# Layer 3's expert results sent to the tokens' rows block by block, and layer 0's attention written in two parts a batch

## The chip, the cores and the metric

The kernel runs on one core of one Trainium2 chip. The metric is device time in microseconds (us) of one execution: the median of several. Engines are named as in the profile: PE (TensorE matmul), PEld (TensorE weight load), DVE (VectorE), ACT (ScalarE), POOL (GpSimd) and SP (SyncE, which here only issues transfers). Each engine runs its instructions in the order in which they stand in its stream.

## The reference

Four layers, each a cross-attention and an expert network, both added to `x` (4 batches of 512 tokens, 128 wide, all float32). The context has 154 rows of 128 a batch. Layer 0's attention and layer 3's experts are what the change rewrites most:

```python
# layer 0: one score matrix, softmax over the context, and one summary of the tokens
Sim = (hc @ w1)[:, :, None] + (hq @ w2)[:, None, :] + einsum('bid,bjd->bij', hc * w3, hq) + b_sim[0]
hq_hat = einsum('bij,bjd->bid', softmax(Sim, axis=2), hq)
hc_bar = einsum('bi,bid->bd', softmax(max(Sim, axis=2), axis=1), hc)[:, None, :]
x = x + concatenate([hc, hq_hat, hc * hq_hat, hc * hc_bar], -1) @ W_qv + b_qv     # hc = layernorm(x), hq = context
# layer 3's experts: 8 experts, the two best of each token, 128 -> 512 -> 128
top_vals, top_idx = top_k(logits, 2)                       # logits = xn @ W_router + b_router
w = softmax(the two values)
out = sum over the token's two experts e of  w[e] * (relu(xn @ W1[e] + b1[e]) @ W2[e] + b2[e])
x = x + out                                                # this is the kernel's output
```

Layers 0 and 2 also send each token to two experts, layer 1 to one. Layers 1 to 3 have attention with 16 heads.

## The kernel before

`x` stays in SBUF, 4 batches with 4 groups of 128 tokens each. The expert networks work in two halves of two batches (1,024 tokens). For a half, `route` (L650 to L807) computes the logits, finds the experts, counts tokens per expert with matmuls of triangular matrices, and gives every (token, choice) a slot `su` so that the tokens of an expert lie together and every expert starts at a multiple of 128. `scatter` (L722) is one indexed transfer of POOL for 128 tokens and one choice: it writes their normalised rows `xn` to the DRAM array `buf` at the slots. With two choices a half has 16 scatters. `experts` (L825 to L946) then runs over blocks of 128 slots: 23 blocks a half where there are two choices, 15 in layer 1. It loads four blocks of `buf` at a time (`tok`, L840), transposes them (L850), loads the weights of the block's expert from DRAM (`w<-in_up`, L862 and L869), multiplies up (L877), applies the activation (L900 to L912), multiplies down (L916), copies the result to `ys` (L925) and stores it to the DRAM array `ybuf` (L928). `gather` (L948) queues 16 indexed reads on POOL (L953), one for 128 tokens and one choice, each of which waits for all stores of its half, and `combine` (L964) adds the rows, times their weights, to `x` (L971).

Indexed transfers are put in a list, `rows_due`, and started by `row_transfers` (L641) from places in the other work, a few at a time; each such place makes them wait for one of its instructions, which spreads them over that work.

The order of the engines' work comes from three sources. Much of it is laid down by a scheduler, which orders the program's instructions for each engine. The attention of layers 1 to 3 (`attend_all`, L1296) is under a manual order: periods, one per 128 tokens, in which PE and ACT (and from layer 2 on DVE) follow the program's order. Generators with `yield` cut `route`, `experts` and the combining of half 1 into steps, which are called from within other work (`Steps`).

The halves overlap: half 1's route runs beside half 0's experts, half 0's gathers beside half 1's experts, half 1's gathers beside the first periods of the next layer's attention. After layer 3 there is nothing beside half 1's gathers.

Layer 0's attention differs: `prepare` (L1002) computes the scores of a batch and `tile_of` (L1026 to L1083) the rest: transposed softmax `pm` and `pt`, the product `hq`, the maximum over all tokens `mall`, the exponentials `ebt`, the summary `hc`, and twelve matmuls with W_qv (L1078) into `res`. `attend_first` (L1278) runs the four batches, with half 0's route after the second and its 16 scatters beside the third and fourth. After it the transposes of layer 1's weights are issued (L1097 to L1108).

In the main loop (L1346 on), SP's queue carries the loads of tokens and weights, the stores to `ybuf`, and in layer 3 the output stores `out_x` (L1392 for half 0, L1403 for half 1).

Of the kernel before, what the change touches and what calls it, by code (L numbers as in the profile page):

```python
# [9 lines left out]
F32 = mybir.dt.float32  # L10
I32 = mybir.dt.int32
# [18 lines left out]
NH = NT // 2  # L30
EPS = 1e-5
NEG = -1e20
BLK = (2 * NH + E - 1, NH + E - 1)
UPS = (2, 1, 1, 1)
NF = (4, 4, 2, 4)
PER = (1, 2, 2, 2)


# [9 lines left out]
def tile_xattn_moe_stack(ctx: ExitStack, tc: tile.TileContext, a: dict, out: bass.AP):  # L48
# [73 lines left out]
    upper = const.tile([P, P], F32, name="upper")  # L122
# [22 lines left out]
    nc.gpsimd.memset(wide_ends, 0.0)  # L145
# [4 lines left out]
    for base, sign in ((0, 1), (D // H - 1, -1)):  # L150
# [17 lines left out]
    fill = const.tile([P, E, NH], F32, name="fill")  # L168
    nc.gpsimd.iota(
        fill, pattern=[[0, E], [P, NH]], base=0, channel_multiplier=0, allow_small_or_imprecise_dtypes=True  # L170
# [6 lines left out]
    nth = const.tile([1, BLK[0], E], F32, name="nth")  # L177
    nc.gpsimd.iota(
        nth, pattern=[[1, BLK[0]], [0, E]], base=0, channel_multiplier=0, allow_small_or_imprecise_dtypes=True
# [59 lines left out]
    def norm(src, found, pool=None):  # L239
        mv, rstd = found  # L240
        xn = (pool or xnp).tile([P, NI, D], F32, tag="xn", name="xn", bufs=3 if pool else 2)
        for i in range(NI):
            nc.vector.tensor_scalar(
                xn[:, i, :], src[:, i, :], mv[:, i, 0:1], rstd[:, i : i + 1], ALU.subtract, ALU.mult
            )
        return xn

    def transposed(xn, gamma=None, beta=None):
        q = ps_tr()
        for i in range(NI):  # L250
            nc.tensor.transpose(q[:, i * P : (i + 1) * P], xn[:, i, :], ident)
# [18 lines left out]
    class Tile:  # L270
# [31 lines left out]
        def exp(self, g):  # L302
            if g == 0:
                self.pr = p2.tile([P, H, S2], F32, tag="probs", name="probs")
            for s in range(min(3, 8 - 3 * g)):
                for j in range(2):
                    h = self.at.heads(None, 3 * g + s, j)
                    nc.scalar.activation(  # L308
# [5 lines left out]
                    )  # L314

        def short(self):
            if self.nb == 1:
                self.ends = p2.tile([P, 4, T4], F32, tag="short", name="short", bufs=1)
# [41 lines left out]
        def take_ends(self, engine):  # L360
            self.tails = p2.tile([self.rows, 4, P], F32, tag="tails", name="tails")
            copy(engine, self.tails.rearrange("p g q -> p (g q)"), self.q["ends"][0 : self.rows, :])
# [173 lines left out]
    def attention64(b, gather_x, wq, wk, wv, wo, add):  # L536
# [36 lines left out]
        def values_ends():  # L573
# [3 lines left out]
            for r in range(2):  # L577
                rows = slice(64 * r, 64 * r + 64)
                nc.tensor.matmul(q[rows, :], ct2[:, b], wv[:, r * 512 : (r + 1) * 512], start=True, stop=True)
# [6 lines left out]
            at.vt = at.vt.rearrange("p c s d -> p (c s d)")  # L586

# [35 lines left out]
    def rsm(name, *shape, dt=F32):  # L623
        return rt.tile([P, *shape], dt, tag=name, name=name)

    def top(lg):

        m = rt.tile([P, NH], F32, tag="m", name="m", bufs=4)
        nc.vector.tensor_reduce(m, lg, AX.X, ALU.max)
        eq = rt.tile([P, NH, E], F32, tag="eq", name="eq", bufs=4)  # L630
        nc.vector.tensor_tensor(eq, lg, bc(m, 2, E), ALU.is_equal)
        nc.vector.tensor_tensor(eq, eq, bc(rev_e, 1, NH), ALU.mult)
        r = rt.tile([P, NH], F32, tag="r", name="r", bufs=4)
        nc.vector.tensor_reduce(r, eq, AX.X, ALU.max)
        oh = rt.tile([P, NH, E], F32, tag="oh", name="oh", bufs=4)
# [5 lines left out]
    def row_transfers(n=2 * NH, behind=None):  # L641
# [5 lines left out]
        del rows_due[:n]  # L647

    seen = []

    def route(layer, half, wg, bg, b2):

        lg = rsm("lg", NH, E)
        found = [stats(x[2 * half + k]) for k in range(B // 2)]
        yield
        xns = [norm(x[2 * half + k], found[k], rt) for k in range(B // 2)]
        yield  # L660
        xnTs = [transposed(xn) for xn in xns]
        yield
        for k, xnT in enumerate(xnTs):
            q = ps_tr()
            for i in range(NI):
                nc.tensor.matmul(q[:, i * E : (i + 1) * E], xnT[:, i * P : (i + 1) * P], wg, start=True, stop=True)
            o = lg[:, k * NI : (k + 1) * NI, :]
            qv = q[:, 0 : NI * E].rearrange("p (i e) -> p i e", i=NI)
            if bg is None:
                nc.vector.tensor_copy(o, qv)  # L670
            else:
                nc.vector.tensor_tensor(o, qv, bc(bg, 1, NI), ALU.add)
        yield
# [3 lines left out]
        sel = rsm("sel", NH + 1, E, dt=BF16)  # L677
        nc.vector.memset(sel[:, NH, :], 0.0)
        if layer == 1:
            nc.vector.tensor_copy(sel[:, 0:NH, :], oh1)  # L680
        else:
            yield
            lg2 = rsm("lg2", NH, E)
# [3 lines left out]
            nc.vector.tensor_tensor(sel[:, 0:NH, :], oh1, oh2, ALU.add)  # L687
# [3 lines left out]
        n = (NH + 1) * E  # L691
        q = ps_tr()
        nc.tensor.matmul(q[:, 0:n], before, sf, start=True, stop=False)
        for s in range(1, NH + 1):
            nc.tensor.matmul(q[:, s * E : n], ones_b, sf[:, 0 : n - s * E], start=False, stop=(s == NH))
        rk = rsm("rk", NH + 1, E)
        nc.vector.tensor_copy(rk, q[:, 0:n].rearrange("p (t e) -> p t e", t=NH + 1))
        tot = rk[:, NH, :]
        t3 = rsm("t3", E, NH)
        nc.vector.tensor_tensor(t3, bc(tot, 2, NH), fill, ALU.is_gt)  # L700
        nb = rsm("nb", E)
        nc.vector.tensor_reduce(nb, t3, AX.X, ALU.add)
        t4 = rsm("t4", E, E)
# [4 lines left out]
        base = rsm("base", NH, E)  # L708
        nc.vector.scalar_tensor_tensor(base, bc(first, 1, NH), float(P), rk[:, 0:NH, :], ALU.mult, ALU.add)
        slots = []  # L710
        for k, oh in enumerate(ohs):
            t5 = rsm("t5", NH, E)
            nc.vector.tensor_tensor(t5, base, oh, ALU.mult)
            sl = rsm(f"sl{k}", NH)
            nc.vector.tensor_reduce(sl, t5, AX.X, ALU.add)
            su = rsm(f"su{k}", NH, dt=U32)
            nc.vector.tensor_copy(su, sl)
            slots.append(su)
        scatters = []

        def scatter(t, su):
            ins = nc.gpsimd.indirect_dma_start(  # L722
                out=buf[half],
# [10 lines left out]
        rows_due.extend(partial(scatter, t, su) for t in range(NH) for su in slots)  # L734
# [698 lines left out]
```

## Time and profile before

| | |
|---|---|
| median of 3 runs | 1352.45 us (1351.14 to 1359.07) |
| the profiled execution | 1282.47 us |
| its span, first to last instruction | 1280.8 us |
| mean granted TensorE clock in it | 0.917 of full speed |
| layer 0: attention; experts | about 20 to 104; 106 to 262 us |
| layer 1: attention; experts | about 260 to 500; to 560 us |
| layer 2: attention; experts | about 560 to 800; to 895 us |
| layer 3: attention; experts | about 895 to 1140; 1144 to 1251 us |
| the end: last `ys` to the end of the span | 1251.4 to 1280.8 us |
| bytes moved by DMA | 126.77 MB, mean 99 GB/s |

The profile is one execution, taken by the hardware profiler. It gives for every engine its busy time and number of instructions; for each group of instructions (a line of the kernel, an engine, an operation, and the tiles it writes and reads, out<-in) the busy time, the mean time of one in ns, the idle time of the engine ahead of it, and what ended most of that; and a chain, followed back from the last instruction to what released each one. In a timeline the first number is the start in us from the beginning of the span, the second the duration. "issue" is time in which an engine waited for nothing that the profile shows; SPq and POOLq are the instruction queues of SP and POOL that issue transfers. The profiled execution is 70 us shorter than the median of the runs.

### The profile page before, as it was taken

Reading aid. Unit: us, or ns where it says so; the run is one execution under the profiler, and the core shown is the slowest. Engines: PE = TensorE matmul, PEld = TensorE weight load, DVE = VectorE, ACT = ScalarE, POOL = GpSimd, SP = SyncE. Lnnn points to the kernel's source line nnn. Section 1 sums busy time; section 2 is a strip of 40 time slices with the busy share of each in tenths; the row PEclk is TensorE's granted clock in tenths of the full one; section 3 lists DMA queues with packets and bytes.
Section 4 is the critical chain, followed back from the end, with each engine's and each line's share of the span. In section 5 each row is a group of like instructions: output and inputs, shape, how many; then the busy total and the mean of one; then the engine's idle time right before and its main releaser. Section 6 shows DMA issues by size and latency. Waiting matters only on the chain.

```text
span 1280.8 us, 26318 instructions
## 1 busy us (share of the span) xinstructions
PE 1089.4 (85%) x9351; PEld 896.9 (70%) x9351; DVE 731.6 (57%) x2012; ACT 565.3 (44%) x2264; POOL 253.6 (20%) x281
## 2 busy tenths in 40 slices
PE   4787998977878888889999998966899999899990
PEld 3657998933435448787878777855778788789890
DVE  6554646567666763335665776424476576646352
ACT  2113433454554543546656565321656665532230
POOL 2041315023000010232000004045220000402334
PEclk8767999988898988998999999887999999999996
DMA  7023786721100314433112214444421111334762
GB/s 228 1 81 113 216 253 189 207 94 25 23 19 26 100 38 119 133 110 84 35 35 55 64 37 123 123 150 133 127 55 45 41 35 35 109 95 143 209 191 60
DMA packets 136064, 126.77 MB, mean 99 GB/s; under 512 B 12538, under 2 KB 115583, under 8 KB 135551
## 3 DMA queue, kind: packets, MB, share of 16 engines
q1 hardware_dynamic: 128767, 110.39, 30.5%
q0 software_dynamic: 7168, 14.69, 3.9%
q8 instruction: 77, 1.26, 0.4%
q14 instruction: 52, 0.43, 0.1%
HBM read 101.31 MB, written 23.72 MB: 98 GB/s over the span
## 4 chain that ended last, share of the span: by engine, by line
PE 59%; DVE 12%; DMA 9%; issue 8%; ACT 5%; POOL 5%; SPq 2%; POOLq 0%; DVEq 0%
PE sc L877 11%; PE av L916 6%; PE tr L371 6%; PE sc L607 5%; PE av L408 5%; PE tr L425 5%; PE sc L592 3%; DMA yg<-ybuf,su 3%; POOL yg L953 3%; ACT probs L308 3%; DVE nm L294 3%; PE sc L1175 2%; DMA w<-in_up 2%; PE av L390 2%; PE tr L358 2%
## 5 line engine op out<-in xcount | busy, mean ns | idle before, releaser
L308 ACT ACTIVATE probs<-sc,nm 128x154 f32<-128x154 f32 x768 | 286.9, 403 | 162.7 <-DVE nm L294 162.5
L877 PE MATMUL sc<-tokT,w 128*128 128x128 f32 x1528 | 201.3, 286 | 8.7 <-DMA w<-in_up 3.6
L877 PEld LDWEIGHTS sc<-tokT,w 128*128 128x128 f32 x1528 | 189.0, 200 | 15.5 <-ACT eg L900 5.2
L294 DVE TENSOR_REDUCE nm<-sc 128x6 f32<-128x924 f32 x144 | 142.6, 1007 | 74.8 <-PE sc L607 49.1
L308 ACT ACTIVATION_READ_ACCUMULATOR probs<-sc,nm 128x1 f32 x768 | 168.3, 219 | 0.0
L916 PE MATMUL av<-w,hT 128*128 x1160 | 155.3, 279 | 3.2 <-DVE hT L905 2.5
L953 POOL DMA_INDIRECT yg<-ybuf,su x112 | 106.7, 952 | 246.5 <-ACT pT L267 59.9
L722 POOL DMA_INDIRECT buf<-xn,su x112 | 109.6, 979 | 227.0 <-DVE eb L745 97.3
L916 PEld LDWEIGHTS av<-w,hT 128*128 128x128 f32 x1160 | 141.9, 193 | 8.9 <-issue 4.7
L236 POOL TENSOR_TENSOR rstd<-ve,nhalf 128x4 f32<-128x4 f32 x32 | 33.0, 1032 | 547.3 <-DVE ve L234 429.6
L264 DVE COPY pT<-tr 128x512 f32<-128x512 f32 x160 | 106.9, 684 | 45.3 <-PE tr L371 41.5
L408 PE MATMUL av<-pT,vm 128*64 128x128 f32 (+1 forms) x1536 | 106.2, 284 | 22.5 <-DVE pT L264 22.4
L371 PE MATMUL tr<-ident,probs 128*128 128x128 f32 x768 | 123.1, 291 | 1.5 <-DVE rT L337 1.5
L371 PEld LDWEIGHTS tr<-ident,probs 128*128 128x128 f32 x768 | 86.1, 146 | 33.4 <-issue 21.7
L408 PEld LDWEIGHTS av<-pT,vm 128*64 128x64 f32 (+1 forms) x1536 | 63.8, 126 | 55.7 <-DVE pT L264 30.9
L900 ACT ACTIVATE eg<-sc,w 128x128 f32<-128x128 f32 x184 | 52.9, 368 | 89.5 <-PE sc L877 82.1
L607 PE MATMUL sc<-kT,qT 64*128 64x154 f32 x1024 | 87.1, 308 | 4.8 <-ACT probs L308 4.8
L905 DVE SCALAR_TENSOR_TENSOR hT<-sc,w,eg 128x128 f32<-128x128 f32 x184 | 56.2, 342 | 51.0 <-ACT eg L900 51.0
L607 PEld LDWEIGHTS sc<-kT,qT 64*128 64x128 f32 x1024 | 71.3, 189 | 15.8 <-issue 9.9
L592 PE MATMUL sc<-xnT,wq 128*128 128x128 f32 x512 | 73.6, 303 | 4.7 <-ACT probs L308 2.3
L592 PEld LDWEIGHTS sc<-xnT,wq 128*128 128x128 f32 x512 | 67.3, 212 | 10.2 <-issue 3.6
L425 PE MATMUL tr<-wo,aT 128*128 128x128 f32 x512 | 66.2, 284 | 1.6 <-DVE xnT L256 1.3
(255 smaller groups left out, 1432.2 us busy)
## 6 DMA issues: line engine op xcount, KB each, us to landing
w<-in_up SPq DMA_DIRECT2D x46, 516.0 KB
w<-in_up SPq DMA_DIRECT2D x76, 258.0 KB
rep<-rd SPq DMA_DIRECT2D x64, 256.0 KB
tok<-buf SPq DMA_DIRECT2D x36, 256.0 KB
ybuf<-ys SPq DMA_DIRECT2D x58, 128.0 KB
w<-in_down SPq DMA_DIRECT2D x3, 2048.0 KB
w<-in_up SPq DMA_DIRECT2D x46, 128.0 KB
ybuf<-ys SPq DMA_DIRECT2D x52, 64.0 KB
```

The lines of the kernel that those rows point to most:

```text
L264: return nc.vector.tensor_copy(o, i)
L294: nc.vector.tensor_reduce(self.at.heads(self.nm, g, n), self.sc[g][:, :, 0 : n * S2].rearrange("p j (s k) -> p j s k", s=n), AX.X, ALU.max ...
L308: nc.scalar.activation(self.pr[:, h, :], self.sc[g][:, j, s * S2 : (s + 1) * S2], AF.Exp, bias=self.nm[:, h : h + 1], accum_out=self.rs[:, ...
L371: nc.tensor.transpose(q[:, t * P : (t + 1) * P], self.pr[:, h, 0:P], ident)
L408: nc.tensor.matmul(av[rows, cols], v, self.pT[n][:, t, :], start=False, stop=last)
L425: nc.tensor.matmul(o[:, 0:D], self.aT[:, c, :], self.at.wo[:, c, :], start=(c == 0), stop=(c == self.nb - 1))
L592: nc.tensor.matmul(sc[:, c // 4, c % 4 * P : (c % 4 + 1) * P], wq[:, c * P : (c + 1) * P], at.xnT[:, i * P : (i + 1) * P], start=True, sto ...
L607: nc.tensor.matmul(sc[:, j, s * S2 : (s + 1) * S2], at.qT[i][rows, c, :], at.kT[rows, c, :], start=True, stop=True)
L722: ins = nc.gpsimd.indirect_dma_start(out=buf[half], out_offset=bass.IndirectOffsetOnAxis(ap=su[:, t : t + 1], axis=0), in_=xns[t // NI][:, ...
L877: nc.tensor.matmul(dst, w[:, b, at : at + P], xT, start=True, stop=True)
L916: nc.tensor.matmul(y[:, b * D : (b + 1) * D], hT[:, fc, :], w2[:, bass.ds(es[b], 1), fc, :].rearrange("p o d -> p (o d)"), start=(fc == 0) ...
L953: ins = nc.gpsimd.indirect_dma_start(out=yg[:, t, :], out_offset=None, in_=ybuf[half], in_offset=bass.IndirectOffsetOnAxis(ap=su[:, t : t ...
```

## The change

It has four parts.

*Layer 3's results.* A row that is sent to the experts is two floats longer in layer 3 (130 instead of 128): the first is the token's row number in an array by tokens, two rows a token, less 4096; the second is the slot of its first choice. These rows go to DRAM arrays of their own, `last`, which are cleared by two more stores at SP. When the experts read a group of blocks, DVE compares the slot in each row with the slot at which it lies (`other` is 1 where it is the token's second choice) and computes `goal`, the row of (token, choice); a slot that no token filled has a goal beyond the array. Each block's `ys` is sent to the rows `goal` of `by_token` by one indexed transfer of POOL with a bounds check, which leaves out the rows beyond the array. These are listed in `results_due` and started up to six pairs of blocks late (`LAG`; layer 3 works on two blocks at a time, and a `ys` holds both), and `ys` has 8 buffers instead of 3. `sums` reads a batch with one plain load of 512 KB at SP, adds both choices to `x`, and stores the output. `ybuf`, its stores, and the gathers fall away in layer 3.

*Layer 0's attention.* `tile_of` is a generator with one `yield` after `ebt`; `attend_first` puts its halves and the steps of half 0's route in a manual order for PE. The route works batch by batch in layer 0. The matmuls of `hq` come after the transpose of the maximum. Each spot starts 4 scatters instead of 2. The route of half 1 has its first step in `attend_first`. The set-up of layer 1's attention (its weights' transposes) comes after half 0's experts instead of ahead of them.

*Gathers of layers 0 to 2.* The gathered rows are in tiles of one batch (6 buffers) instead of a half (2), and a batch's sums follow when its own gathers have been started. In layer 1's first period each group of exponentials starts three gathers, and the second period takes a step of the combining.

*Buffers.* Fewer buffers for several small tiles of the route and for `tails`; four for the normalised rows of the route; one tile for layer 0's gates; `short` shares the memory of `wide_ends`, whose clearing moves to after layer 1's attention; in layer 1 the parts that prepare the next batch's keys and queries come one period later.

The core of the diff:

```diff
@@ experts
+        loaded, toks, goals = {}, {}, {}
+        buf = bufs[layer == 3][half]
...
+            if layer == 3:
+                other = small.tile([P, 4], F32, tag="other", name="other")
+                nc.vector.tensor_tensor(
+                    other[:, 0:m], tok[:, 0:m, D + 1], slot[:, 4 * g : 4 * g + m], ALU.not_equal
+                )
+                goal = small.tile([P, 4], U32, tag="goal", name="goal", bufs=6)
+                nc.vector.scalar_tensor_tensor(
+                    goal[:, 0:m], tok[:, 0:m, D], float(ROWS), other[:, 0:m], ALU.add, ALU.add
+                )
+                goals[g] = goal
...
-            ys = p3.tile([P, 2, D], F32, tag="ys", name="ys")
-            row_transfers(
-                2 * n, nc.vector.tensor_copy(ys[:, 0:n], y[:, 0 : n * D].rearrange("p (b d) -> p b d", b=n))
+            ys = p3.tile([P, 2, D], F32, tag="ys", name="ys", bufs=LAG + 2)
+            done = nc.vector.tensor_copy(ys[:, 0:n], y[:, 0 : n * D].rearrange("p (b d) -> p b d", b=n))
+            some = min(len(rows_due), 2 * n)
+            row_transfers(some, done)
+            if layer == 3:
+                results_due.extend(partial(result, j, ys[:, b, :]) for b, j in enumerate(blocks))
+                results(4 - some)
+                results(len(results_due) - LAG * n)
+            else:
+                rows = ybuf[half][blocks[0] * P : (blocks[0] + n) * P, :]
+                stores.append(nc.sync.dma_start(rows.rearrange("(b p) d -> p b d", p=P), ys[:, 0:n]))
+
+        def result(j, y):
+            ins = nc.gpsimd.indirect_dma_start(
+                out=by_token[half],
+                out_offset=bass.IndirectOffsetOnAxis(ap=goals[j // 4][:, j % 4 : j % 4 + 1], axis=0),
+                in_=y,
+                in_offset=None,
+                bounds_check=ROWS - 1,
+                oob_is_err=False,
             )
-            rows = ybuf[half][blocks[0] * P : (blocks[0] + n) * P, :]
-            stores.append(nc.sync.dma_start(rows.rearrange("(b p) d -> p b d", p=P), ys[:, 0:n]))
...
@@ after gather and combine
+    def sums(half, routed, stores):
+        batches = GROUPS[3][half]
+        def get(b):
+            yg = p2.tile([P, NI, 2, D], F32, tag="k", name="yg2")
+            rows = by_token[half][2 * b * S : 2 * (b + 1) * S, :].rearrange("(i p c) d -> p i c d", p=P, c=2)
+            wait_for(nc.sync.dma_start(yg, rows), stores, "any block may hold these tokens")
+            return yg
+        for k, yg in enumerate([get(b) for b in batches]):
+            b = batches[k]
+            for i in range(NI):
+                t = k * NI + i
+                xi = x[b][:, i, :]
+                for c, (cw, _) in enumerate(routed[1]):
+                    nc.vector.scalar_tensor_tensor(xi, yg[:, i, c, :], cw[:, t : t + 1], xi, ALU.mult, ALU.add)
+            nc.sync.dma_start(out_v[b], x[b])
+            yield
...
@@ Tile.exp
+            if self.at.dh < 64 and self.at.first and self.i == 0:
+                row_transfers(3, ins)
...
@@ attend_first
-        tiles = [prepare(b, found[b]) for b in range(2)]
-        tiles[0](0)
-        tiles.append(prepare(2, found[2]))
-        tiles[1](0)
-        beside = Steps(route(layer, 0, *gates[layer])).step(3)
-        tiles.append(prepare(3, found[3]))
-        beside.step(5)
-        tiles[2](0)
-        beside.step(1)
-        tiles[3](0)
-        return beside.finish()
+        first, second = (Steps(route(layer, half, *gates[layer])) for half in range(2))
+        with tc.manual_schedule(engines={mybir.EngineType.PE}):
+            tiles = [prepare(b, found[b]) for b in range(2)]
+            tiles[0].finish()
+            tiles.append(prepare(2, found[2]))
+            tiles[1].step()
+            first.step()
+            tiles[1].finish()
+            tiles.append(prepare(3, found[3]))
+            tiles[2].step()
+            first.step(3)
+            tiles[2].finish()
+            first.step(2)
+            tiles[3].step()
+            first.step(2)
+            tiles[3].finish()
+            first.finish()
+            second.step()
+        return first.result, second
...
@@ main loop
+        if layer == 3:
+            second = Steps(experts(layer, 1, routed[1], w2))
+            while len(stores) < most_blocks(layer, 0):
+                second.step()
+            got = Steps(sums(0, routed[0], stores))
+            while not (second.done and got.done):
+                second.step(2)
+                got.step()
+            results()
+            Steps(sums(1, routed[1], second.result)).finish()
+            break
+        got = gather(layer, 0, routed[0], stores)
+        if layer == 0:
+            prepare = setups[1]()
+        at = prepare(0, found)
```

## The prediction

> **What bounds the kernel now.** I read the page from the top: engine shares, the chain that ended last, then the costliest groups; after that the chain by time, the timeline and the busy time by stretch for the three places that the change touches.
>
> ```profile
> PE 1089.4 (85%) x9351; PEld 896.9 (70%) x9351; DVE 731.6 (57%) x2012; ACT 565.3 (44%) x2264; POOL 253.6 (20%) x281
> ...
> PE 59%; DVE 12%; DMA 9%; issue 8%; ACT 5%; POOL 5%; SPq 2%; POOLq 0%; DVEq 0%
> ...
> L953 POOL DMA_INDIRECT yg<-ybuf,su x112 | 106.7, 952 | 246.5 <-ACT pT L267 59.9
> L722 POOL DMA_INDIRECT buf<-xn,su x112 | 109.6, 979 | 227.0 <-DVE eb L745 97.3
> ```
>
> TensorE carries 59% of the chain, and its work is all but unchanged. What can move is the rest, and it sits in few places: POOL's 5% is nearly all gathers. One indexed transfer occupies POOL 0.95 us, and the timeline has the next start 1.25 us (gather) or 1.265 us (scatter) later. The end of the chain by time:
>
> ```profile
> 1249.28 1.80 PE av L916 x16
> 1251.43 2.79 DMA ybuf<-ys
> 1254.68 0.49 issue
> 1255.38 0.95 POOL yg L953
> 1256.63 0.94 POOL yg L953
> ...
> 1273.83 0.30 issue
> 1274.13 2.40 DMA yg<-ybuf,su
> 1276.63 0.35 DVE x L971
> ```
>
> TensorE is done at 1251.1; then a store, 16 gathers in a row, one landing, a multiply-add and the output store: 1280.8 - 1251.4 = 29.4 us with TensorE idle. The busy times by stretch (busy and number of PE, PEld, DVE, ACT, POOL; granted clock; DMA share; GB/s) say the same, and show the two other places:
>
> ```profile
> 75.00:100.00 25.00, 23.76 (x107) 18.86 (x107) 11.27 (x43) 2.33 (x7) 13.99 (x15) 0.59 0.28 99
> ...
> 270.00:305.00 35.00, 22.38 (x178) 10.85 (x178) 26.18 (x72) 15.84 (x78) 16.39 (x17) 0.94 0.15 38
> ...
> 1200.00:1250.00 50.00, 47.23 (x391) 45.93 (x392) 23.99 (x77) 14.11 (x47) 15.20 (x16) 0.97 0.74 216
> 1250.00:1281.00 31.00, 1.07 (x10) 0.88 (x8) 6.77 (x20) 0.00 (x0) 15.13 (x16) 0.60 0.21 58
> ```
>
> Layer 0's attention (75 to 100) runs TensorE busy but at clock 0.59; layer 0 to 1 (270 to 305) leaves TensorE idle 12.6 of 35 us beside 16 gathers; the last experts (1200 to 1250) are full, but DMA is at 0.74.
>
> **What the Trainium skill says.** "DMA: Bandwidth & Descriptors", section "Anatomy of one DMA", puts a fixed cost of about 2 us on each DMA, most of it the receipt of the write. The trace agrees: last gather 2.40 us from issue to use, last scatter before layer 0's experts 2.25. Its section "Issuing engines are not separate DMA queues" says that DMAs of SP and POOL run on the same 16 engines: result scatters compete with the weight loads of the last experts, which at 0.74 have a quarter left. Its section "How a descriptor splits into AXI transactions" counts more beats for rows that don't begin at 256 B: 520-byte rows do so; no run here shows such rows. "TensorE: Matmul & The Clock Gate", Part 1, has the clock at half after an idle window of about 3.4 us; the 0.59 above and the 0.60 of the tail fit.
>
> **Part 1: layer 3's tail.** Gone: 28 SP stores ybuf<-ys and 32 gathers. New: 46 result scatters (23 a half) on POOL, four loads of 512 KB on SP, 24 DVE operations on four columns (nearest: 0.15 to 0.2 us each, 4 us together, beside a DVE that is idle half of that stretch: 24.0 busy of 50). A result with a bounds check is in no row of this trace; the nearest is L722 with 0.96 busy and 1.265 apart. Lower bound: rows out of bounds are dropped, say 0.9; upper: half as much again, 1.9 apart. I take 1.265. Experts give a block every 2.0 to 2.3 us (23 in 46.3 us, PE 1204.6 to 1250.9), so POOL keeps up at 1.265 and just at 1.9.
> After the last ys, the instruction order leaves the last pair or so of results (3 x 1.265 = 3.8), a landing 2.4, the two loads (1 MB together; tok loads of 256 KB take 2.7 to 2.8, so 4 to 6), multiply-adds of the second batch (8 x 0.35 = 2.8) and the output store 3.8: 16.8 to 18.8 instead of 29.4. **Saved: 10.6 to 12.6.**
>
> **Part 2: what it costs ahead of the tail.** POOL between the halves now runs 10 results, 12 scatters, 2 results, 4 scatters. Before, the 16 scatters ran 1177.0 to 1197.0 without a hole, and the chain goes through the last one (1196.05), its landing and tok's load (1198.44, 2.84). Two results in between: 2 x 1.265 = 2.5; rows of 520 B: 0 to 1, I take 0.5. So the second half's experts start 3 us later. Then SP: the loads yg2 of half 0 wait for all 23 results (last issued near 1212.7, landed near 1215) and stand in SP's order ahead of the expert weights of later blocks; the two output stores stand there as well. Behind them: w<-in_up, then TensorE. Before, this place wasn't free either: the chain runs gathers, x L971, SPq L1392, w<-in_up from 1213 to 1233, some 4 us of TensorE idle time. I take 1 us more than before, between -2 (half 0's sums are ready sooner than gathers that end at 1232.8) and +6. **Cost: 4 us (1 to 10). Layer 3 net: -7.5 (-12 to 0).**
>
> **Part 3: layer 0's attention.** TensorE's order is written by hand, and half 0's route is spread over it. The number of matmuls stays. Before, a tile took 13 to 15 us, the route sat between 54.6 and 72.3 with TensorE often idle (14.6 busy of the 25 us from 50 to 75), and tile 3 ended at 98.5. I estimate 86 for tile 3 after: the 10.4 idle us filled, and some 2 us from an earlier start. But the experts wait for the 16 scatters, not for tile 3: first scatter 72.78, last 101.17 with the end in 103.4. In the new order the slots `su` come after tile 2 instead of before it; counting DVE's work ahead of them, near 81. From there 16 x 1.265 = 20.2, landing 2.3: 103.5 to 104. **The gain is swallowed: 0,** between -8 (su at 73 and no spreading) and +4 (su behind tile 3's work on DVE). Layer 1's weight transposes (L1099 to L1108) move behind half 0's experts; in the chain they held wo_r's load for 1.8 us at 91.84, which is part of the gain that scatters hide. The first steps of half 1's route also move ahead of the experts, under the scatters.
>
> **Part 4: layer 0 to 1.** The 16 gathers of half 1 ran from 274.1 to 301.1, spread by their order; three are now issued at each exp group of the first tile. Their condition, stores ending at 269.2, stays. 16 x 1.25 = 20 from there: the last starts at 288 and not 300. TensorE's idle time of 4.5 us before L358 at 304.76, for the residual behind x L971, should go; but DVE, in order, takes the combines in front of the second tile's maxima, and waits for gathers there instead, up to about 6 us. Net -1.5 (-6 to +4). Layers 1 to 2 and 2 to 3 keep their order; per-batch tiles let batch 0's sums go earlier: 0 (-2 to +1).
>
> **Costed at nothing.** Two more clears of 1.5 MB on SP's queue, in the 32 us slice that moved 1 GB/s near 32 to 64, before the first expert weights at 73: cover 30 us; without it, 3 MB at about 200 GB/s would delay weights by 15 us. Fewer buffers (eq, tails, route tiles): each is written again a tile later, 12 us on; gone cover would show as DVE waits of about 0.3 us. memset of wide_ends moves to POOL after layer 1's attention, where it is idle.
>
> **Sum.** -7.5 + 0 - 1.5 - 0.5 (a bit of Part 3's earlier work) = -9.5 us on the profiled execution of 1282.47 (span 1280.8 and 1.67 around it). That lies 70 us below the median of 1352.45. What I change is idle time set by DMA and POOL, which a slower TensorE does not stretch, so I carry over microseconds and not a ratio: 1352.45 - 9.5 = **1343 us.**
>
> **Rivals.**
> 1. *Forecast (0.50):* tail shortened, the rest about even: -4 to -13.
> 2. *All parts pay (0.28):* su comes near 74, so that layer 0's experts start 7 us sooner, and layer 1's start gains its 4.5: -8 - 7 - 4 = -19, 1333. For it: 10.4 us of idle TensorE in 50 to 75. Against it: 20 us of scatters on POOL remain after su.
> 3. *Slower (0.17):* SP's queue stalls the last experts. If half 0's results land late (price 1.9 apart: 23 results and 16 scatters take 64 us from 1157, to 1221 and later), yg2's loads and the output stores hold the weights behind them, each w load being 4 us from issue to use. It decides from a stall of about 12 us, three weight pairs late one after the other; with 16 us lost, and layer 1's combines 5 us late, it is +10: 1362. For it: SPq is in the chain there already, DMA 0.74 busy. Against it: three pairs of weights are loaded ahead.
> 4. *The tail doesn't shorten (0.05):* results lag, and POOL holds 10 of them at the end: 12.6 us instead of 3.8, leaving 2 us of gain, about 1350.
>
> A measurement of this kernel can tell about 1% (13.5 us) from no change. Forecast -9.5 lies inside this; of case 1 about a quarter lies beyond -13.5, with the sizes' errors, of case 2 nearly all: faster by over 1% 0.38, within 0.51, slower 0.11. Range: down to 1328 for case 2 with its bounds, up to 1359 to take in most of case 3.
>
> **What would show it.** Right: after the last ys, at most four result scatters, two loads and the store in 16 to 19 us; the first experts' tok load at 103 to 105 although tile 3 ends before 90; gathers of layer 0's half 1 in one row from 269 to 289. Wrong: experts of layer 0 starting before 99; PE idle for more than 8 us in 1205 to 1255 with SP holding w<-in_up behind yg2; result scatters over 1.3 us apart; DVE waiting over 8 us for gathers at layer 1's start.

## The result, and the profile after

The changed kernel is slower: 1363.59 us (median of 20 runs, 1351.95 to 1377.62) against 1353.8 (20 runs, 1342.29 to 1360.08), ratio 1.0078, interval 1.0058 to 1.0098. The prediction had 1343 (1328 to 1359). A ratio here is the time of a kernel over that of the kernel before in the same set of runs, with its 95% interval.

Sets of runs on different chips came at two levels of time: the kernel before took 1355.0 us (median) on the chip that the record numbers 10, 1278.4 and 1280.1 on chips 12 and 14, and the set above, whose chip isn't recorded, is of the upper level; the profile that the prediction was read from (span 1280.8) is of the lower. The ratio of the changed kernel is the same at both (a second set, at the lower level, gave 1.0080 with 1.0054 to 1.0107), but the places where it loses are not quite the same. The profiles below are of the lower level unless the text says otherwise.

The page of the changed kernel, in the parts shown of before:

```profile
PE 1084.9 (85%) x9351; PEld 893.2 (70%) x9351; DVE 730.4 (57%) x2044; ACT 564.9 (44%) x2264; POOL 267.9 (21%) x297
...
PE 54%; DVE 15%; issue 10%; DMA 9%; POOL 5%; ACT 5%; SPq 0%; POOLq 0%; DVEq 0%; ACTq 0%
```

TensorE's busy time is within 0.5% of before, but its share of the chain fell from 59% to 54%. DVE's share rose from 12% to 15% with its busy time unchanged: DVE is more often the one that the others wait for. The tail, by the chain in order of time:

```profile
1264.69 0.98 POOL by_token L1007
...
1268.65 2.12 DMA by_token<-ys,goal
...
1270.99 3.45 DMA yg<-by_token
1274.44 0.03 issue
1274.46 3.50 DVE x L1092 x13
```

From the last result to the end of the span it is what was forecast: three results, a landing, two loads, sums, the store; 16.1 us from the last ys instead of 29.7. These 13.6 us are gained. What is lost ahead of it, the time from one kind of block to the next shows. Each entry is the time from the row above, taken at the first and last `ys` copy (DVE) of each half of experts (h0, h1); "changed" is its second profiled execution, and the last three columns are experiments:

| to | before | changed | late goals | + scatters first | + no early gathers |
|---|---|---|---|---|---|
| layer 0, end of h1 | 261.7 | 264.3 | 262.3 | 264.5 | 262.4 |
| layer 1, start of h0 | 229.9 | 230.4 | 228.6 | 234.7 | 225.0 |
| layer 1, end of h1 | 82.5 | 85.6 | 85.1 | 89.0 | 88.1 |
| layer 2, end of h1 | 332.3 | 331.2 | 331.5 | 331.8 | 331.7 |
| layer 3, start of h0 | 249.9 | 254.6 | 248.1 | 248.1 | 248.0 |
| layer 3, end of h0 | 48.6 | 44.9 | 43.8 | 48.8 | 48.8 |
| layer 3, start of h1 | 7.5 | 16.8 | 16.8 | 6.1 | 6.0 |
| layer 3, end of h1 | 38.7 | 38.5 | 38.9 | 41.2 | 41.2 |
| end of the span | 29.7 | 16.1 | 16.7 | 16.5 | 16.4 |

The profiles of before and of the changed kernel are 1.6 us apart and not 10: the changed one is the shortest of its six runs, the one of before lies 2 to 4 us above the medians of its level. In the same way "late goals" is the shortest of its 11 runs and "+ scatters first" one of the longest of its 22. What differs by several us between executions with the same code is the first three rows, so they are not read alone; the layer 3 rows repeat within 0.6 us in a second profile of the kernel before at this level (`before_third`, below). In them the tail gains 13.6, and the four rows ahead of it lose 10.1: layer 3 is 3.5 us ahead, where 7.5 was forecast, and layers 0 to 2 are behind, by 5.2 us in these two profiles and by more in the medians.

At the upper level layer 3's loss sits elsewhere: its half 0 takes 65.9 us in the changed kernel's first profile and 53.8 in a kernel that has layer 3's results as before (`l3_old`, below); the three other rows ahead of the tail add up to less than 1 us, and the tail gains 12.5. In that half DVE has two waits, of 8.5 and 9.6 us, that the profile puts down to something "remote"; `l3_old` has one of 8.7, on ACT. What that is stays open (last section).

```profile
1252.83 1.13 DVE L979 TENSOR_SCALAR hT<-sc,w 128x128 f32<-128x128 f32 x4 [8.47 <-remote]
1271.76 1.13 DVE L979 TENSOR_SCALAR hT<-sc,w 128x128 f32<-128x128 f32 x4 [9.56 <-remote]
```

Two waits stand out in the changed kernel. From the table of waits, engine, line and what it waited for, with total us, times, longest:

```profile
DVE other L913 <- DMA tok<-last: 22.3, 10, 6.0
```

And DVE's timeline in the last periods of layer 3's attention:

```profile
1135.12 0.69 DVE L286 COPY pT<-tr 128x512 f32<-128x512 f32 x1
1139.84 0.16 DVE L913 TENSOR_TENSOR other<-tok,slot 128x4 f32<-128x4 f32 x1 [4.02 <-DMA tok<-last]
1139.91 0.68 DVE L286 COPY pT<-tr 128x512 f32<-128x512 f32 x1
1140.52 0.15 DVE L917 SCALAR_TENSOR_TENSOR goal<-tok,other 128x4 uint32<-128x4 f32 x1
```

and TensorE's:

```profile
1136.48 0.66 PE L395 MATMUL tr<-ident,probs 128*128 128x128 f32 x4
1140.65 1.12 PE L432 MATMUL av<-pT,vm 128*64 128x128 f32 x8 [3.52 <-DVE pT L286]
```

The goal's first instruction takes 0.16 us and waits 4.02 us for the load of the rows (3.31 us, from 1136.50), which itself waits for the last scatter (1133.99, landed after 2.37). Behind it in DVE's order stands a copy of the attention (`pT`), and for that TensorE waits 3.52 us. It is most of the 4.7 us more in the row "layer 3, start of h0". The second wait is on POOL, between the halves:

```profile
1203.36 0.96 POOL L777 DMA_INDIRECT last<-rows,su  x1 [0.30 <-issue]
1204.62 0.99 POOL L1007 DMA_INDIRECT by_token<-ys,goal  x1 [0.30 <-issue]
1205.92 0.98 POOL L1007 DMA_INDIRECT by_token<-ys,goal  x1 [0.31 <-issue]
1207.20 0.96 POOL L777 DMA_INDIRECT last<-rows,su  x1 [0.30 <-issue]
...
1210.99 0.95 POOL L777 DMA_INDIRECT last<-rows,su  x1 [0.30 <-issue]
```

Twelve scatters, two results, four scatters: half 1's rows are complete only after the last scatter. TensorE's first transpose of them, in the kernel before and in the changed one:

```profile
1201.32 0.91 PE L850 MATMUL tr<-ident,tok 128*128 128x128 f32 x4 [2.39 <-DMA tok<-buf]
1217.23 1.97 PE L906 MATMUL tr<-ident,tok 128*128 128x128 f32 x8 [6.31 <-DMA tok<-last]
```

### The profile page after: what moved, and what is told of

It is laid out like the page before. It is cut to its first block, busy times and chain, and to the rows that moved or that the text cites. A ratio compares the mean times of both kernels' runs of the same rounds, so it can differ in the third digit from the quotient of the medians.

```text
span 1350.0 us, 26336 instructions
## 1 busy us (share of the span) xinstructions
PE 1107.2 (82%) x9351; PEld 904.4 (67%) x9351; DVE 728.3 (54%) x2044; ACT 564.8 (42%) x2264; POOL 268.9 (20%) x297
## 4 chain that ended last, share of the span: by engine, by line
PE 55%; DVE 16%; issue 10%; DMA 8%; ACT 5%; another core or an unknown queue 4%; POOL 2%; SPq 1%; POOLq 0%; DVEq 0%; ACTq 0%
PE sc L944 10%; PE av L985 7%; PE tr L395 6%; PE av L432 5%; PE sc L632 5%; PE tr L449 4%; ACT probs L330 3%; DVE nm L316 3%; PE sc L1300 2%; PE sc L617 2%; DMA w<-in_up 2%; PE av L414 2%; DMA yg<-ybuf,su 2%; PE tr L382 2%
## 5 line engine op out<-in xcount | busy, mean ns | idle before, releaser
L944 PE MATMUL sc<-tokT,w 128*128 128x128 f32 x1528 | 205.1, 287 | 20.5 <-DMA w<-in_up 8.1
L985 PE MATMUL av<-w,hT 128*128 x1160 | 165.5, 287 | 31.0 <-issue 21.2
L985 PEld LDWEIGHTS av<-w,hT 128*128 128x128 f32 x1160 | 148.6, 198 | 40.6 <-issue 26.0
L432 PE MATMUL av<-pT,vm 128*64 128x128 f32 (+1 forms) x1536 | 109.1, 287 | 28.0 <-DVE pT L286 25.9
L1050 POOL DMA_INDIRECT yg<-ybuf,su x80 | 77.1, 964 | 219.7 <-issue 62.0
L777 POOL DMA_INDIRECT buf<-rows,su x80 | 77.6, 970 | 167.5 <-DVE ve L255 54.9
L432 PEld LDWEIGHTS av<-pT,vm 128*64 128x64 f32 (+1 forms) x1536 | 64.4, 128 | 63.2 <-DVE pT L286 38.1
L632 PE MATMUL sc<-kT,qT 64*128 64x154 f32 x1024 | 88.8, 312 | 4.8 <-ACT probs L330 4.8
L993 DVE COPY ys<-av 128x256 f32<-128x256 f32 (+1 forms) x110 | 38.8, 355 | 84.8 <-PE av L985 43.1
L974 DVE SCALAR_TENSOR_TENSOR hT<-sc,w,eg 128x128 f32<-128x128 f32 x184 | 56.1, 342 | 45.4 <-ACT eg L969 45.3
L449 PE MATMUL tr<-wo,aT 128*128 128x128 f32 x512 | 70.8, 296 | 2.4 <-DVE xnT L278 1.3
```

The lines of the kernel that those rows point to most:

```text
L432: nc.tensor.matmul(av[rows, cols], v, self.pT[n][:, t, :], start=False, stop=last)
L449: nc.tensor.matmul(o[:, 0:D], self.aT[:, c, :], self.at.wo[:, c, :], start=(c == 0), stop=(c == self.nb - 1))
L632: nc.tensor.matmul(sc[:, j, s * S2 : (s + 1) * S2], at.qT[i][rows, c, :], at.kT[rows, c, :], start=True, stop=True)
L777: ins = nc.gpsimd.indirect_dma_start(out=bufs[layer == 3][half], out_offset=bass.IndirectOffsetOnAxis(ap=su[:, t : t + 1], axis=0), in_=xn ...
L944: nc.tensor.matmul(dst, w[:, b, at : at + P], xT, start=True, stop=True)
L985: nc.tensor.matmul(y[:, b * D : (b + 1) * D], hT[:, fc, :], w2[:, bass.ds(es[b], 1), fc, :].rearrange("p o d -> p (o d)"), start=(fc == 0) ...
```

## The experiments

**The kernel before, once more** (`before_again`), and a third time among the last runs (`before_third`), for profiles. No edit.

> The kernel before, unchanged, for a second profiled execution. Its 20 runs lie between 1342 and 1360 us, and the execution that the prediction was read from took 1282 us. Theory 'the profile was an exception': a second execution takes 1340 to 1360 us, and the 60 to 70 us more lie in stretches where DVE and ACT stand still together while POOL issues a row of indexed transfers (layers 2's and 3's experts, each 10 to 20 us), which the change then inherits. Rival 'profiling makes it faster': it takes about 1282 again, with the stages of the first profile.

It took 1352.48 us, span 1350.8: the first profile was of another level, not an exception within one. Part of the 70 us lies where expected: layer 2's first half of experts takes 48.4 us from first to last ys at the upper level and 30.6 at the lower. But of these 17.8 us the wait for half 1 behind it makes 9.1 good (11.0 us instead of 20.1). The largest difference is from layer 2's last ys to layer 3's first: 268.8 us instead of 249.9.

> The kernel before once more, for a profile on the chip of these runs: 1353 or 1280 us, as the chip is; the stages are compared with the three kernels above.

It took 1286.02 us; layer 3's rows were 249.9, 48.2, 8.0, 38.1 and 29.9 us, as in the first profile.

**One part undone at a time.** Layer 3's results as before (`l3_old`), the early gathers taken out (`exp_old`), layer 0's attention as before (`l0_old`).

```diff
 # exp_old
-            if self.at.dh < 64 and self.at.first and self.i == 0:
-                row_transfers(3, ins)
 # l0_old
-        for some in ([b] for b in batches) if layer == 0 else (batches,):
+        for some in (batches,):
...
+        tiles[0].finish()
+        tiles.append(prepare(2, found[2]))
+        tiles[1].finish()
+        beside = Steps(route(layer, 0, *gates[layer])).step(3)
+        tiles.append(prepare(3, found[3]))
+        beside.step(5)
+        tiles[2].finish()
+        beside.step(1)
+        tiles[3].finish()
```

> The changed kernel with layer 3's results by ybuf stores and gathers as before; all else as changed. Theory 'layer 3 costs': time falls by about 10 us or more against the changed kernel, to the kernel before (1350 to 1355). Rival 'layer 3 pays 7.5 us as predicted and the other parts cost 18': about 1371. Rival 'layer 3 neutral': 1361 to 1366.

> The changed kernel without the three gathers at each exp group of layer 1's first tile, so that half 1's gathers of layer 0 start with the sums and the later copies. Theory 'early gathers put waits in front of the second tile's maxima on DVE': about 5 us faster than the changed kernel, 1357 to 1360. Rival 'they pay as predicted, 1.5 us or more': 1364 to 1369.

> The changed kernel with layer 0's attention as before: scheduler's order on PE, half 0's route in one piece after the second batch, two scatters a spot, layer 1's transposes ahead of the experts. Theory 'layer 0's gain is swallowed by the scatters': within 4 us of the changed kernel. Rival 'the new order pays': 5 to 8 us slower than the changed kernel. Rival 'it costs': 5 us faster or more.

Measured, ratios to before at the upper level: `l3_old` 1.0056 (1.0033 to 1.0080), `exp_old` 1.0051 (1.0029 to 1.0073), `l0_old` 1.0059 (1.0040 to 1.0079), against 1.0078 for the change. The intervals of all four overlap, so none of the parts carries the loss alone. For layer 3 a loss of 10 us is excluded, and so is the forecast gain of 7.5: undoing it brings 3 us, give or take 4. The tail of `l3_old` is 29.0 us where that of the changed kernel's first profile is 16.5, and the stretches ahead of it are shorter by as much. For the early gathers the 3.6 us lie between the two theories and decide for neither. For layer 0 nothing is to be seen of a gain or a loss, as expected.

**Two parts undone, and the changed kernel again** at the lower level.

> The changed kernel, unchanged, on the chip and in the hours of the next runs, and for a second profiled execution, since its first was the shortest of its 20. Expected 1361 to 1366 us, ratio to before 1.006 to 1.009, and by stages: 239 us from layer 0's last expert block to layer 1's first (as two other kernels with the early gathers show), 66 to 68 us for layer 3's first half, a tail of 17 us.

> The changed kernel without the early gathers in layer 1's first tile and with layer 3's results by ybuf and gathers. Theory 'the early gathers cost 10 us in layer 1's start and layer 3 is even': within 3 us of the kernel without the early gathers alone, and within 4 us of the kernel before. Rival 'both parts cost, each a little': 1356 and less, 5 us below the kernel without the early gathers. Rival 'something else in the change costs (buffers, gathers by batch)': it stays 5 to 7 us above the kernel before.

The changed kernel gave 1.0080; its stage times are in the table, and the stretch expected at 239 us was 230.4, since that number was one of the upper level. With both parts undone (`exp_l3_old`) the ratio is 1.0016 (0.9995 to 1.0037): what remains of the change is within 5 us of the kernel before. That fits more than one of the theories. But the profiles show layer 3 alone, since the two kernels have the same code otherwise but for the early gathers: from layer 2's last ys to the end they take 370.9 us (changed) and 370.3. The tail gains 12.4 and half 0 takes 3.6 less; half 0 begins 6.7 later, half 1 another 9.3, and half 1 takes 0.5 more. What was done to layer 3's results is even, as a gain and a loss of about 16 us each, and the loss can be mended if its cause is known. (Layer 3 is still 3.5 us ahead of the kernel before, because something in the other parts shortens it by 4.1: it takes 374.4 there.)

**Half 1's results direct, half 0's by gathers** (`half1_direct`, also without the early gathers).

```diff
-        buf = bufs[layer == 3][half]
+        direct = layer == 3 and half == 1
+        buf = bufs[direct][half]
...
-            if layer == 3:
+            if direct:
                 results_due.extend(partial(result, j, ys[:, b, :]) for b, j in enumerate(blocks))
```

> The changed kernel without the early gathers; layer 3's results go straight to the tokens' rows in half 1 only, while half 0 keeps ybuf stores and 16 gathers. Theory 'the 10 result scatters between and beside half 1's token scatters cost 12 us in half 0': half 0's experts back at 54 to 56 us, the tail still 17 to 20 us, total 6 to 12 us below the changed kernel without early gathers: 1349 to 1355, level with or below the kernel before. Rival 'POOL has 39 transfers beside half 1's experts and lags': the tail stays at 25 us or more, or half 1 takes 10 us longer, and the total does not fall.

1.0002 (0.9980 to 1.0024). The time from layer 2's last ys to half 0's first was back at 247.9 us and the time between the halves at 8.2, so both delays do come from half 0's new code. But POOL now has 16 gathers and 23 results beside half 1: that half takes 41.6 us, and the tail 22.3. Both theories were half right.

**A layer's scatters left out** (`no_l2_scatter`): 16 scatters of layer 2's half 1 are left out, so its experts read old rows.

```diff
-        rows_due.extend(partial(scatter, t, su) for t in range(NH) for su in slots)
+        if (layer, half) != (2, 1):
+            rows_due.extend(partial(scatter, t, su) for t in range(NH) for su in slots)
```

> The kernel before, with the 16 token scatters of layer 2's second half left out (its experts read old rows; nothing else is left out). Theory 'a row of POOL transfers holds up the other engines': layer 2's first half takes 28 to 32 us between its first and last ys, as in the short first profile, instead of 48 to 49 as in every execution of usual length. Rival 'something else in that stretch, such as weight loads, holds it up': it stays at 45 us or more.

It ran at the lower level, where this stretch takes 30.6 us anyway (here 32.8), so it doesn't tell the theories apart. It shows something else: the time from half 0's last ys to half 1's first fell from 20.1 to 5.9 us. Layer 2 waits some 14 us there for its scatters; the changed kernel, with 19.9 us at this place, has not changed that.

**The goals computed later** (`goal_late`). The two instructions come after the copy of the group's first result, held there by a wait on it; one more buffer for the loaded rows.

```diff
@@ tokens
             toks[g] = tokT
+            raw[g] = m, tok
-            if layer == 3:
-                other = small.tile([P, 4], F32, tag="other", name="other")
...
@@ down
             row_transfers(some, done)
             if layer == 3:
+                g = blocks[0] // 4
+                if g not in goals:
+                    m, tok = raw.pop(g)
+                    other = small.tile([P, 4], F32, tag="other", name="other")
+                    first_of = nc.vector.tensor_tensor(
+                        other[:, 0:m], tok[:, 0:m, D + 1], slot[:, 4 * g : 4 * g + m], ALU.not_equal
+                    )
+                    wait_for(first_of, (done,), "after the work that waits")
...
```

> The changed kernel, in which DVE computes the goals of a group of blocks after the copy of the group's first result instead of right behind the group's load (one more buffer for the loaded rows). Theory 'the goal instructions stand in DVE's order ahead of the last attention period and wait there for the first load of rows': the stretch from layer 2's last ys to layer 3's first falls from 254.6 to 248-250 us (or from 274 to 269-270 on a chip where the whole takes 1350), and the total by 4 to 7 us against the changed kernel: ratio to before 1.003 to 1.005. Rival 'rows of 520 bytes are the cost': the stretch stays.

1.0029 (1.0009 to 1.0048), and 248.1 us for the stretch: the theory holds. The rival of the 520-byte rows falls, since the rows are as long as in the changed kernel. None of the twelve goal pairs waits for a load any more. The added buffer was not tried alone. DVE's timeline at the same place:

```profile
1128.95 2.15 DVE L316 TENSOR_REDUCE nm<-sc 128x6 f32<-128x924 f32 x2 [1.20 <-PE sc L632]
1131.21 1.29 DVE L286 COPY pT<-tr 128x512 f32<-128x512 f32 x2
1133.33 0.69 DVE L286 COPY pT<-tr 128x512 f32<-128x512 f32 x1 [0.83 <-PE tr L395]
```

The longest hole among the copies is now 0.83 us.

**Scatters ahead of results** (`goal_late_sfirst`). Half 0's results that come after half 1's scatters in the program wait for the same copy as these, so that the scheduler doesn't draw two of them forward.

```diff
+            if layer == 3 and some:
+                cleared[0] = done
...
+            if half == 0 and cleared[0] is not None:
+                wait_for(ins, (cleared[0],), "after the other half's rows")
```

> As the kernel with late goals, and half 0's later results stand behind all 16 token scatters of half 1 in POOL's order (6 results, 16 scatters, 17 results). Theory 'results ahead of the scatters make half 1's experts late': the time between layer 3's first and second half (last ys of half 0 to first of half 1) falls from 17 to 9-13 us and the total by another 3 to 6 us; the tail may grow by up to 3 us. Rival 'the delay only moves to the tail': total within 2 us of the kernel with late goals alone.

0.9976 (0.9959 to 0.9993). POOL's order is as wanted, and TensorE's first transpose of half 1's rows comes after the load that follows the last scatter:

```profile
1207.72 0.96 POOL L777 DMA_INDIRECT last<-rows,su  x1 [0.30 <-issue]
1208.98 0.99 POOL L1012 DMA_INDIRECT by_token<-ys,goal  x1 [0.30 <-DMA last<-rows,su]
...
1213.36 1.11 PE L906 MATMUL tr<-ident,tok 128*128 128x128 f32 x4 [2.47 <-DMA tok<-last]
```

The time between the halves fell from 16.8 to 6.1 us, more than expected. Against that half 0 took 5 us longer and half 1 2.3, which wasn't expected. So the rows of layer 3 gain 3.5 in these profiles and the medians 0.53% (6.8 us, give or take 3), and the tail stays at 16.5. The whole is now faster than before.

**And without the early gathers** (`mended`, the edit of `exp_old` on top).

> As the last, without the early gathers in layer 1's first tile. Theory 'the early gathers cost 3 to 4 us': ratio to before 0.990 to 0.996, the best of all. Rival 'they cost nothing': within 2 us of the kernel with them.

0.9938 (0.9913 to 0.9962): 1271.12 us, the best of all, 0.6% (8 us) below the kernel before and 1.4% below the change. The early gathers cost 0.38%, about 5 us, give or take 4 (0.27% in the pair at the upper level). What they do is seen on DVE in layer 1's first periods, in the changed kernel:

```profile
267.93 0.80 DVE L316 TENSOR_REDUCE nm<-sc 128x4 f32<-128x616 f32 x1 [1.15 <-PE sc L1300]
270.66 0.25 DVE L354 RECIPROCAL rinv<-rs 128x16 f32<-128x16 f32 x1 [1.94 <-ACT probs L330]
275.56 0.35 DVE L1074 SCALAR_TENSOR_TENSOR x<-yg,wa,x 128x128 f32<-128x128 f32 x1 [4.65 <-DMA yg<-ybuf,su]
275.83 1.11 DVE L316 TENSOR_REDUCE nm<-sc 128x6 f32<-128x924 f32 x1
```

and in the mended one:

```profile
268.80 0.25 DVE L352 RECIPROCAL rinv<-rs 128x16 f32<-128x16 f32 x1 [1.93 <-ACT probs L330]
268.97 1.06 DVE L316 TENSOR_REDUCE nm<-sc 128x6 f32<-128x924 f32 x1
270.39 1.12 DVE L316 TENSOR_REDUCE nm<-sc 128x6 f32<-128x924 f32 x1 [0.36 <-PE sc L1305]
276.85 0.35 DVE L1079 SCALAR_TENSOR_TENSOR x<-yg,wa,x 128x128 f32<-128x128 f32 x1 [1.96 <-DMA yg<-ybuf,su]
```

With the gathers early the scheduler puts the first sum ahead of the second tile's first maxima (`nm`). The sum waits 4.65 us for its gather. The exponentials of ACT wait 5.78 us for the maxima, and TensorE waits 7.37 us for a small copy (`rT`) that stands behind the sums in DVE's order:

```profile
276.98 0.39 ACT L330 ACTIVATE probs<-sc,nm 128x154 f32<-128x154 f32 x1 [5.78 <-DVE nm L316]
281.75 1.11 PE L395 MATMUL tr<-ident,probs 128*128 128x128 f32 x4 [7.37 <-DVE rT L361]
```

Without them two maxima go first, and ACT waits 0.72 us.

## Why the prediction was wrong

By its own terms, in us at the lower level (1% is 12.8). The ratios of the last three experiments take the change apart: 1.0080 to 1.0029 to 0.9976 to 0.9938; each step between them is uncertain by some 0.3% (4 us), and the first joins sets from two chips.

- *The tail, "Saved: 10.6 to 12.6".* Right, slightly small: 29.7 to 16.1, 13.6. Results with the bounds check are 1.285 us apart (1.265 taken), three are left at the end as forecast, and scatters of 520-byte rows are 1.265 apart, like those of 512. (24 stores fell away, not 28: `ybuf<-ys` has 110 before and 86 after.)
- *"24 DVE operations ... beside a DVE that is idle half of that stretch".* **This is the step that failed.** It priced the new instructions by their duration, 4 us, hid that under idle time, and so put the term at nothing. Their duration was right (0.16 us each, 3.9 together). But each pair waits for a load, and ten of the twelve waited 22.3 us together in DVE's in-order stream. The longest wait, 6.0 us, cost nothing more, since TensorE waited for the same load. The first, 4.02 us, stood in front of a copy that the last attention period needed. The prediction asked for neither the wait nor the place of these instructions. Measured by putting them later: 6.5 us in the row "layer 3, start of h0" (254.6 to 248.1; it is 247.8 to 248.1 in the five variants of the changed kernel that lack the goals there), and 0.51%, 6.5 us, in the medians.
- *"Two results in between: 2 x 1.265 = 2.5".* The order was read rightly and the kind of cost too, but it was taken as 3 us of a later start plus 1 for SP. Counted from half 0's first ys, half 1's first came after 61.7 us instead of 56.1: 5.6 later. (The row "start of h1" shows 9.3, because half 0 ended 3.7 sooner.) The two results are 2.6 of it, as forecast. Another 2.6 are that the scatters began later, 23.4 us after half 0's first ys (1189.46) instead of 20.8 (1177.01), which the sum doesn't have; the trace has the first of them waiting for the route's `eb` on DVE, as before. And the last scatter landed in 3.02 us instead of 2.24. Putting the scatters first brings 0.53%, 6.8 us, against the 4 of the sum.
- *SP's queue, rival 3.* Not the cause. The loads of half 0's sums do stand ahead of weights (the chain has one w<-in_up of 4.54 us at 1229), but half 1 takes 38.5 us, as before, and at the upper level 41.4, where the kernel before takes 48.4.
- *Layer 0, "The gain is swallowed: 0".* Right, by its mechanism: the slots came at 82.92 and 83.65 (forecast 81), the last tile ended at 88.45 (86), and the last scatter went out at 102.52 with tok's load behind it. TensorE idles ahead of the first transpose:

```profile
107.84 1.09 PE L906 MATMUL tr<-ident,tok 128*128 128x128 f32 x4 [13.35 <-DMA tok<-buf]
```

  In the third profile of the kernel before:

```profile
107.48 1.97 PE L850 MATMUL tr<-ident,tok 128*128 128x128 f32 x8 [6.75 <-DMA tok<-buf]
```

  The prediction puts the granted clock of 0.59 in layer 0's attention down to an idle window. Nothing in the sum rests on that, but it was misread. An idle window fits the tail, where the granted clock is 0.5 from 1256.2 us on, after TensorE's last work. It doesn't fit the attention: from 75.2 to 88.8 us the clock was 0.5 as well, but TensorE's only wait of over 1 us between 70 and 88 was one of 1.15.
- *Layer 0 to 1, "Net -1.5 (-6 to +4)".* Both halves of it were named, and the balance was wrong. The 4.5 us of idle time before L358 did go: at the same place (L382, 299.20) TensorE waits 0.77 us. The gathers end sooner, but not in one row: the last starts at 294.33 instead of 300.15, where 288 was forecast. The wait on DVE came in its place, and it holds TensorE for 7.37 us. Without the early gathers the time falls by 4.9 us, so the sign was wrong, and the size lies just outside the stated bounds.
- *The carry-over.* The prediction took the 70 us between profile and median for a slower TensorE. The granted clocks of the two levels, 0.917 and 0.905 in the profiles, are 1.3% apart, and the times 5.5%, so the clock explains a quarter of it at most. As the ratio is the same at both levels, this was not what failed.

The three steps take the changed kernel from +10.3 (0.80%, where -9.5 was forecast) to -7.9, and account for 18.2 us. These are 6.5 more than forecast for the goals, 2.8 more for the order of results and scatters, and 6.4 more for the gathers: 15.7 of the 19.8 us between forecast and result. The tail gains up to 3 us more than forecast, so some 5 to 7 us of loss remain that no step explains; this is rough, as each step is uncertain by 4. They seem to lie in layers 0 to 2: with both the early gathers and layer 3's results undone (`exp_l3_old`) the kernel is still 2.0 us above before (-0.6 to 4.7), though its layer 3 is 4.1 us shorter in the profile. Which of the other parts costs them, the smaller buffers among these, is open. The 2 us of fixed cost that the Trainium skill's "DMA: Bandwidth & Descriptors" gives in "Anatomy of one DMA" are there again (2.12 us from the last result to its landing), but the loss lay elsewhere.

## What to carry to other kernels

A cheap instruction that reads something loaded is priced by its place in its engine's order, not by its duration: ask what it waits for, and which instruction stands behind it when it does. Where the order is not written by hand, as for the goals and the results here, a scheduler may draw such an instruction, or a transfer that is ready early, ahead of the one that others need; a dependence on the last instruction of the urgent group kept it back in both cases. Starting transfers earlier did not help here, because their readers moved ahead with them.

## What was not expected of the hardware

At the upper level of time some stretches in which POOL issues a row of indexed transfers take longer. In the second profile of the kernel before, beside 16 scatters of layer 2 (857 to 877 us), the copies of results wait for something that the profile names "remote":

```profile
859.89 0.42 DVE L925 COPY ys<-av 128x256 f32<-128x256 f32 x1 [0.39 <-issue]
...
866.60 0.42 DVE L925 COPY ys<-av 128x256 f32<-128x256 f32 x1 [6.28 <-remote]
...
880.15 0.76 DVE L925 COPY ys<-av 128x256 f32<-128x256 f32 x2 [13.12 <-remote]
```

The matmuls for the second of these copies and for one of the last two end by 863.5 in the record, and at the lower level the same copies come every 1.8 us beside the same scatters. The first periods of layer 3's attention, beside 16 gathers, are longer too: from the first `rinv` to the fourth it takes 56.4 us there and 44.5 at the lower level. But in layer 1's attention, also beside 16 gathers, it takes 26.3 and 27.5 from the first to the third, so the transfers alone don't do it. What holds the engines up there is open: the run that left scatters out came at the lower level. So is why it happens in some sets alone. The upper level came on chip 10 and the lower on chips 12 and 14, but no chip is recorded in two sets.
